# Four graph-attention layers on one core: reordering the opening, PE transposes for entry 1, and new due times

## The chip, the cores and the metric

The kernel runs on one core of one Trainium2 chip. The metric is the device time of one launch in microseconds. The profile that is quoted is one execution of the program, taken by the hardware profiler. PE is the matmul engine, PEld its weight load, DVE the vector engine, ACT the scalar engine, POOL the GpSimd engine, SP the engine whose queue issues most DMAs.

## What is computed

The input `x` has 16 entries of 1024 nodes with 256 features; `adj` is one 1024 x 1024 adjacency matrix for all of them. Four layers follow one another, each of this form:

```
h = relu(layernorm(x))
x = x + activation(softmax(mask(scores(h))) @ (h @ W))
```

Layers 0 and 3 have four heads of 64 features, and their scores are `leaky_relu(s_src + s_dst)` with two numbers per node and head. Layer 1 is the same with one head of 256. Layer 2 has full products `(h W1)(h W2)^T` as scores. Layers 0, 1 and 3 end with elu, layer 2 with relu.

## The kernel before

Everything is fp32. The weight of a pair of nodes is factored, so that the exponential of a leaky relu becomes a maximum of a row value and a column value: one DVE instruction (L1117 for layers 0 and 3, L1208 for layer 1) makes one *p tile*, 128 keys x 512 queries, masked by the transposed adjacency (`mask`, four quarters). PE multiplies it with the values: for a head of layers 0 and 3 into `acc` (eight key tiles, 16 narrow matmuls of 65 columns in the trace for each tile), for layers 1 and 2 into `accb` (257 columns). Layer 2's tiles come from a PE product (`qT`, `hT`, 512 columns), two exponentials on ACT (L1235, L1236) and two DVE instructions (L1240, L1241). One entry has 128 tiles of p for layers 0 and 3 together, 16 for layer 1 and 16 for layer 2.

Before each layer stands a prologue: statistics on DVE (L822, L823), the reciprocal root as a POOL power (L858), `nshift` on DVE (L861), normalised tiles `h` on ACT (L891), their transposes, the projection with the layer's weight on PE, and its eviction on ACT (L972, L975, L977 or L983 on DVE). The transposes go one of two ways. In the usual way ACT splits `h` into 16-bit planes (L914), a DMA turns them (L918), and ACT puts them together (L932). In the *direct* way PE turns `h` as fp32 tiles (L906) and ACT copies them (L929); there, too, the rows of row values come by PE from one column each (L1025) and an ACT copy (L1029), not through DRAM (L1051, L1064). Before, entry 0's layer 0 and the last entry's layer 3 go the direct way.

No engine's order is written by hand. Each step is given to a `Plan` with an engine, a cost, a due time, the steps it follows and the buffers it takes; the plan simulates the engines and, for each of them, picks the step with the earliest due time among those that are ready. What comes out is the order in which instructions are issued; at run time, engines wait on one another's semaphores, not on the plan. Due times are in periods of 190 us: `START` for a layer's tiles, `LEAD` for how long ahead its prologue is due, `STEP` between its pairs of tiles, `WHEN` for layers 1 and 2, and `LATER` and `AHEAD` for single entries near both ends. Buffers matter too: 8 of p, 18 of p1 (layers 1 and 2), 5 of x (the four adjacency quarters take four of them at the start), 2 each of `acc` and `accb`, 1 of `o`.

The program opens with the loads of entry 0's x in three parts (L636, on SP), the four adjacency quarters of 1 MB (L729, on SP), and w0 with its a vectors on ACT's queue (L654, L664). w0 gets extra columns (DVE, L674, L684, L697) for the scores, and the adjacency becomes the mask: compare (L737, DVE), transpose (PE, L595), copy (L750).

Of the kernel before, what the change touches and what calls it, by code (L numbers as in the profile page):

```python
# [44 lines left out]

PERIOD, EARLY = 190.0, 0.7407
START = {0: 0.0, 1: 1.0372, 2: 2.297, 3: 3.5524}  # L50
LEAD = {0: 0.7046, 1: 0.4612, 2: 0.2956, 3: 1.6786}
STEP = {0: 0.01, 1: 0.0686, 2: 0.0892, 3: 0.0445}
WHEN = {
    (1, "weights"): ((-0.5242, 0.0026), (-0.1464, 0.0419)),
    (1, "attended"): ((0.7567, 0.0147), (0.2574, 0.106)),
    (2, "weights"): ((-0.0331, 0.0103), (0.3531, 0.0135)),
    (2, "attended"): ((0.642, 0.0926), (0.4636, 0.0079)),
}

LATER = {  # L60
    (1, 0): 0.596, (1, 1): 0.958, (13, 2): 0.03, (13, 3): 0.392, (14, 3): -0.089, (0, 2): -0.137, (12, 2): 0.2,
    (13, 1): -0.61, (13, 0): 0.042, (0, 1): 0.165, (14, 2): 0.012, (12, 3): 0.381, (15, 2): 0.061,
    (14, 1): 0.153, (0, 3): -0.204, (0, 0): 0.005, (15, 1): 0.169, (3, 0): -0.106, (3, 2): -0.226,
    (3, 1): -0.037, (3, 3): 0.253, (14, 0): -0.403, (15, 3): 0.422, (12, 0): 0.216, (2, 2): -0.002,
    (2, 3): -0.052, (12, 1): -0.053, (1, 3): 0.022,
}
AHEAD = {
    (1, 0): 0.818, (15, 3): 0.338, (12, 1): 1.914, (15, 1): 0.404, (1, 3): -1.162, (0, 3): 0.168,
    (14, 2): 0.163, (14, 1): -0.3, (1, 1): -0.058, (0, 2): 0.142, (13, 1): 0.271, (3, 1): 0.197, (14, 3): 0.426,
    (3, 3): -0.404, (2, 2): 1.115, (15, 0): -0.042, (12, 0): 0.12, (1, 2): 0.321, (2, 3): -0.168,  # L70
    (3, 2): -0.354, (2, 1): -0.221, (13, 3): -0.364, (0, 1): 0.057, (12, 3): 0.014, (0, 0): -0.016,
    (13, 2): -0.254,
}
# [466 lines left out]
def fast(  # L540
# [16 lines left out]
    nc = tc.nc  # L557
    B, N, F = x.shape
    NT = N // P
# [85 lines left out]
    def weight(w, name, due, a=None, heads=0, own=1):  # L645


        t = const.tile([P, KC, F + 2 * heads], F32, name=name)

        first = name == "w0"  # L650
        queue, engine = (nc.scalar, ACT) if first else (nc.sync, SP)

        def load():
            queue.dma_start(out=t[:, :, :F], in_=w.rearrange("(c p) f -> p c f", p=P))  # L654

        s = landed(plan.add(engine, 0.5, due, load), due, 256)
        if a is None:
            return t, s
        d = F // heads
        tiles = {}  # L660

        def load_a():
            tiles["a"] = buf("p1", [P, own, 2, d], name="a_bc")
            queue.dma_start(  # L664
                out=tiles["a"].rearrange("p h s d -> p (h s d)"),
                in_=bass.AP(tensor=a.tensor, offset=a.offset, ap=[[0, P], [1, own * 2 * d]]),
            )

        s2 = landed(plan.add(engine, 0.5, due, load_a, take=("p1",)), due, own * d)

        def sign():
            for side, by in enumerate((1.0 - SLOPE, SLOPE - 1.0)):
                of = tiles["a"][:, :, side, :]
                nc.vector.tensor_scalar(of, of, by, None, op0=OP.mult)  # L674

        s2 = plan.add(DVE, 0.4, due + 0.5, sign, (s2,))
        done = []
        for c in range(KC):

            def columns(c=c):  # L680
                wa = tiles["wa", c] = buf("u", [P, heads, 2, d], name="wa")
                for side in range(2):
                    of = tiles["a"][:, :, side, :]
                    (nc.vector if first else nc.gpsimd).tensor_mul(  # L684
                        wa[:, :, side, :],
                        t[:, c, :F].rearrange("p (h d) -> p h d", h=heads),
                        of if own == heads else of.to_broadcast([P, heads, d]),
                    )

            m = plan.add(*((DVE, 0.7) if first else (POOL, 2.0)), due + 0.5, columns, (s, s2, *done), take=("u",))  # L690
            done = []
            for hd in range(1 if first else heads):

                def add_up(c=c, hd=hd):
                    wa, to = tiles["wa", c], t[:, c, F:].rearrange("p (s h) -> p h s", s=2)
                    if first:
                        nc.vector.tensor_reduce(to, wa, AX.X, OP.add)  # L697
                        return
                    for side in range(2):
                        junk = small.tile([P, F], BF16, name="junk_a", bufs=1)[:, :d]  # L700
                        nc.scalar.activation(
                            junk, wa[:, hd, side, :], AF.Identity, accum_out=to[:, hd, side : side + 1]
                        )

                give = () if not first and hd < heads - 1 else ("u", "p1") if c == KC - 1 else ("u",)
                done.append(
                    plan.add(*((DVE, 0.6) if first else (ACT, 1.1)), due + 0.5, add_up, (m, *done[-1:]), give=give)
                )
        return t, done[-1]

    first_x = load_x(0, SOON)

# [3 lines left out]

    w0, w0_ready = weight(w_l0, "w0", SOON, a_l0, 4, 4)
    plan.add(ACT, 1.6, SOON, warm)
    plan.add(DVE, 0.2, SOON, lambda: nc.vector.tensor_copy(ident_b, ident))

    def mask_steps():
        done = {}
        for n, (half, jh) in enumerate(((0, 0), (0, 1), (1, 0), (1, 1))):
            due, quarter = 15.0 + n if half else SOON + n, {}

# [4 lines left out]

            loaded = landed(plan.add(SP, 0.9, due, load, take=("x",)), due, 1024)
            for t in range(HT):
# [5 lines left out]

                s = plan.add(DVE, 0.45, due, positive, (loaded,), take=("h",), give=("x",) if t == HT - 1 else ())

# [10 lines left out]

                s = plan.add(*((ACT, 0.6) if half else (DVE, 0.45)), due, keep, (s,), give=("pp",))
                done.setdefault((half, jh), []).append(s)
# [11 lines left out]
    def w12_steps(due):  # L765
        tiles, last = {}, []
        for k, w in enumerate((w1_l2, w2_l2)):
# [4 lines left out]

            loaded = landed(plan.add(SP, 0.5, due, load, take=("p1",)), due, 256)
            for cc in range(KC):
# [53 lines left out]
    class Layer:  # L828
# [7 lines left out]
        def prologue(self, due, step, stats, direct=False):  # L836
# [12 lines left out]
            for n, its in enumerate(slice(*part) for part in parts):  # L849
# [28 lines left out]

                at = due - (len(parts) - n - 1)
                s = plan.add(DVE, 0.2, at, norm, (*stats[its], ready[-1] if n else None))  # L880
                s = plan.add(POOL, 2.0, at, norm2, (s,))
                take = () if n else (tag,) if self.gat else (tag, "hq")
                ready += [plan.add(DVE, 0.2, at, norm3, (s,), take=take)] * (its.stop - its.start)
            copies, evicted = [], []
            for n, t0 in enumerate(range(0, NT, 2)):
# [37 lines left out]
                def kept(t0=t0):  # L923
                    if self.gat:
                        T["hT", t0] = buf("hTp", [P, KC, 2 * P])
                    else:
                        T["hT", t0] = self.hT[:, :, t0 * P : (t0 + 2) * P]
                    if direct:
                        nc.scalar.copy(T["hT", t0], T["tp", t0])  # L929
                        return  # L930
# [3 lines left out]
                take = ("hTp",) if self.gat else ()  # L934
                if direct:
                    s = plan.add(PE, 0.47, at, turned, (s,), take=("pp",), give=("h", "h"), wide=True)
# [8 lines left out]
                for k in range(2):  # L945
# [40 lines left out]
                    cost = 0.32 if many or not self.gat else 0.65 if heads == 1 else 1.05  # L986
                    s2 = plan.add(ACT, cost, at, evict, (s2,), give=() if many else ("pp",))
                    if many:
                        s2 = plan.add(DVE, 0.43, at, scaled, (s2,), give=("pp",))
# [27 lines left out]
            if direct:  # L1017
                for half in range(2):
                    for hd in range(heads):
# [7 lines left out]
                        def keep(half=half, hd=hd):  # L1027
# [3 lines left out]
                        s = plan.add(  # L1031
                            PE, 0.44, at + (half * heads + hd) * 0.01, spread, tuple(evicted[half * HT : (half + 1) * HT]),
                            take=("pp", f"row{heads}"), wide=True,
                        )
                        self.row_ready[half, hd] = plan.add(ACT, 0.6, at, keep, (s,), give=("pp",))
                return
# [16 lines left out]

            s = plan.add(PE, 0.14, at, factors, tuple(evicted), take=("pp",))
            s = plan.add(ACT, 0.35, at, keep, (s,), give=("pp",))
# [336 lines left out]
    for start, b, layer in sorted(order):  # L1392
# [5 lines left out]
        elif b:  # L1398
            loads[b] = load_x(b, due - 0.45 * PERIOD, tuple(lays[b - 1, 0].ready))
            stats = [statistics(b, t, due, (loads[b][t],)) for t in range(NT)]  # L1400
        else:
            due, step = SOON, 0.1
            stats = [statistics(b, t, due - 2.5 + t // 2 * 0.9, (loads[b][t],)) for t in range(NT)]
        lay.prologue(due, step, stats, direct=(b, layer) in ((0, 0), (B - 1, 3)))
# [70 lines left out]
```

## Time and profile before

| | |
|---|---|
| median of 3 runs | 2980.43 us (2977.99 to 2980.48) |
| span of the profiled run | 2977.1 us |
| mean clock granted to PE | 0.993 |
| PE busy | 2911.8 us, 98% |
| DVE busy | 2645.6 us, 89% |
| ACT busy | 1922.3 us, 65% |
| p tiles of layers 0 and 3 (L1117) | 2048, 768 ns each |
| 65-column matmuls on them | 32768 |

A busy share is a mean over stages with different limits. What a change at the opening is worth has to be read from the opening, from which engine waits there and for what. Times in the timeline count from the start of the span.

### The profile page before, as it was taken

Reading aid. Unit: us, or ns where it says so; the run is one execution under the profiler, and the core shown is the slowest. Engines: PE = TensorE matmul, PEld = TensorE weight load, DVE = VectorE, ACT = ScalarE, POOL = GpSimd, SP = SyncE. Lnnn points to the kernel's source line nnn. Section 1 sums busy time; section 2 is a strip of 40 time slices with the busy share of each in tenths; the row PEclk is TensorE's granted clock in tenths of the full one; section 3 lists DMA queues with packets and bytes.
Section 4 is the critical chain, followed back from the end, with each engine's and each line's share of the span. In section 5 each row is a group of like instructions: output and inputs, shape, how many; then the busy total and the mean of one; then the engine's idle time right before and its main releaser. Section 6 shows DMA issues by size and latency. Waiting matters only on the chain.

```text
span 2977.1 us, 108647 instructions
## 1 busy us (share of the span) xinstructions
PE 2911.8 (98%) x47954; PEld 2321.2 (78%) x47954; DVE 2645.6 (89%) x5286; ACT 1922.3 (65%) x4776; POOL 234.5 (8%) x151
## 2 busy tenths in 40 slices
PE   7899999999999999999999999999999999999997
PEld 5776868779697887878779787786877869796876
DVE  8989988899898899989899898988999999797698
ACT  6767776785655767566775656766656684656543
POOL 2111100000000000000000100000000010000001
PEclk9899999999999999999999999999999999999999
DMA  4422223333232333313233232331413332121210
GB/s 130 94 55 59 66 48 97 69 63 74 47 71 58 69 73 59 80 40 84 48 66 77 48 78 44 74 71 38 92 40 70 76 63 57 41 57 35 52 36 25
DMA packets 344048, 188.06 MB, mean 63 GB/s; under 512 B 268880, under 2 KB 304400, under 8 KB 343568
## 3 DMA queue, kind: packets, MB, share of 16 engines
q1 hardware_dynamic: 343152, 180.51, 27.1%
q8 instruction: 378, 6.19, 0.9%
q14 instruction: 102, 0.84, 0.1%
q10 hardware_dynamic: 416, 0.52, 0.1%
HBM read 98.63 MB, written 17.33 MB: 39 GB/s over the span
## 4 chain that ended last, share of the span: by engine, by line
PE 84%; DVE 12%; ACT 1%; issue 1%; DMA 0%; POOL 0%; SPq 0%; DVEq 0%; POOLq 0%
PE pp L582 31%; PE accb L582 27%; PE acc L582 26%; DVE p L1117 8%; DVE o L1088 1%; DVE bn L822 1%; DVE xt L1090 0%; DVE p L1241 0%; DVE mv L823 0%; DVE p L1240 0%; DMA xt<-in_x_dram 0%; ACT hTp L932 0%; POOL xt L1097 0%; DMA turned<-planes 0%; DVE rden L1150 0%
## 5 line engine op out<-in xcount | busy, mean ns | idle before, releaser
L1117 DVE SCALAR_TENSOR_TENSOR p<-row,ke,mask 128x512 f32<-128x512 f32 x2048 | 1460.3, 768 | 34.2 <-PE acc L582 32.6
L582 PEld LDWEIGHTS acc<-val,p 128*64 128x64 f32 x32768 | 1072.4, 139 | 121.6 <-issue 47.3
L582 PE MATMUL acc<-val,p 128*64 128x65 f32 x32768 | 1074.5, 223 | 38.9 <-DVE p L1117 33.8
L582 PE MATMUL accb<-val,p 128*64 128x257 f32 x8192 | 928.0, 380 | 0.0
L582 PEld LDWEIGHTS accb<-val,p 128*64 128x64 f32 x8192 | 734.4, 136 | 131.6 <-issue 4.1
L582 PE MATMUL pp<-qT,hT 128*64 128x512 f32 x2048 | 461.4, 592 | 0.0
L582 PE MATMUL pp<-w,hTp 128*64 128x264 f32 (+1 forms) x3072 | 380.8, 386 | 3.3 <-ACT hTp L932 2.1
L582 PEld LDWEIGHTS pp<-qT,hT 128*64 128x64 f32 x2048 | 171.1, 137 | 211.9 <-issue 209.2
L582 PEld LDWEIGHTS pp<-w,hTp 128*64 128x64 f32 x3072 | 242.5, 137 | 85.2 <-issue 12.0
L891 ACT ACTIVATE h<-xt,nshift,rstd 128x256 f32<-128x256 f32 x512 | 275.5, 596 | 38.2 <-DVE nshift L861 38.2
L1240 DVE SCALAR_TENSOR_TENSOR p<-u,p 128x512 f32<-128x512 f32 x256 | 175.7, 686 | 127.5 <-ACT p L1236 127.1
L1275 ACT ACTIVATE o<-accb,rdens 128x256 f32<-128x256 f32 x128 | 60.5, 473 | 346.9 <-DVE rdens L1267 340.5
L914 ACT COPY planes<-h 128x512 uint16<-128x512 uint16 x496 | 281.8, 621 | 0.0
L932 ACT COPY hTp<-turned 128x1024 uint16<-128x1024 uint16 x184 | 214.2, 1168 | 30.0 <-DMA turned<-planes 29.9
L822 DVE BATCH_NORM_STATS2 bn<-xt 128x6 f32<-128x256 f32 x512 | 211.8, 414 | 13.3 <-DMA xt<-in_x_dram 5.4
L1235 ACT ACTIVATE u<-pp 128x512 f32<-128x512 f32 x256 | 152.9, 597 | 104.7 <-PE pp L582 79.3
L1164 ACT ACTIVATE o<-acc,rden 128x64 f32<-128x64 f32 x572 | 132.2, 316 | 113.4 <-DVE rden L1150 99.9
L858 POOL TENSOR_TENSOR rstd<-rstd,neg_half 128x8 f32<-128x8 f32 (+2 forms) x67 | 124.5, 1858 | 976.0 <-DVE rstd L855 643.2
L1241 DVE TENSOR_TENSOR p<-p,mask 128x512 f32<-128x512 f32 x256 | 179.2, 700 | 8.8
L1097 POOL TENSOR_TENSOR xt<-xt,o 128x1024 f32<-128x1024 f32 x35 | 97.5, 2785 | 1131.7 <-DVE o L1088 1009.6
L1208 DVE SCALAR_TENSOR_TENSOR p<-row,ke,mask 128x512 f32<-128x512 f32 x256 | 180.2, 738 | 0.6 <-DMA row<-er_d 0.5
L977 ACT ACTIVATE val<-pp,val 128x64 f32<-128x64 f32 (+1 forms) x640 | 179.4, 347 | 0.0
(87 smaller groups left out, 1911.7 us busy)
## 6 DMA issues: line engine op xcount, KB each, us to landing
row<-er_d SPq DMA_DIRECT2D x272, 256.0 KB, 3.6
xt<-in_x_dram SPq DMA_DIRECT2D x31, 512.0 KB, 4.8
out_dram<-xt SPq DMA_DIRECT2D x31, 512.0 KB, 3.4
raw<-in_adj_dram SPq DMA_DIRECT2D x4, 1024.0 KB, 15.6
raw<-in_adj_dram SPq DMA_DIRECT2D x16, 256.0 KB, 3.4
turned<-planes SPq DMA_TRANSPOSE x248, 3.2
xt<-in_x_dram SPq DMA_DIRECT2D x2, 256.0 KB
w<-in_L_gnn_W_dram SPq DMA_DIRECT2D x2, 256.0 KB
```

Source lines behind the costliest of these rows:

```text
L582: nc.tensor.matmul(to[c : c + COLS], stationary[:, c : c + COLS], moving, start=start, stop=stop, skip_group_check=True,)
L822: nc.vector.bn_stats(st, x_tiles[b][:, t, :])
L891: nc.scalar.activation(h, x_tiles[b][:, t, :], AF.Relu, bias=T["shift"][:, t : t + 1], scale=T["rstd"][:, t : t + 1],)
L914: nc.scalar.copy(to[:, :, :, k, :], of)
L932: nc.scalar.copy(bits, T["tp", t0].rearrange("p s c q -> p c q s"))
L977: nc.scalar.mul(to[:, hd, :], of[:, hd, :], a[:, hd, :])
L1117: nc.vector.scalar_tensor_tensor(p, lay.rows[half, hd], lay.ke[:, lay.heads + hd, jt : jt + 1], mask_of(half, jt), op0=OP.max, op1=OP.mult)
L1164: nc.scalar.mul(to[:, t, :], acc[:, t, :d], rden[:, t, :])
L1208: nc.vector.scalar_tensor_tensor(p, lay.rows[half, 0], lay.ke[:, 1, jt : jt + 1], mask_of(half, jt), op0=OP.max, op1=OP.mult)
L1235: nc.scalar.activation(u, e, AF.Exp, scale=1.0 - SLOPE)
L1240: nc.vector.scalar_tensor_tensor(p, u, 1.0, p, op0=OP.max, op1=OP.mult)
L1241: nc.vector.tensor_mul(p, p, mask_of(half, jt))
```

## The change

It has five parts.

1. The opening is ordered anew: x is due ahead of all else, the function table of ACT is loaded before w0, the adjacency and the later weights come after x in the plan, and entry 0's norms are due earlier. The costs given for POOL's power, the mask's steps and two others are set anew.
2. The second half of w0's score columns is multiplied on POOL, not on DVE.
3. Entry 1's layer 0 is turned on PE as fp32 tiles, as entry 0's is (its rows still go through DRAM, its values are still scaled on ACT).
4. Rows and row factors depend, in the plan, on the step that makes the factors, and no longer on the scaling of the values after it; in the direct way the first half's rows are due earlier.
5. With these, all due times are searched anew.

The aim is an opening in which PE gets work sooner, and a schedule that fits it. The diff, cut to its core:

```diff
+TURNED_ON_PE = ((0, 0), (1, 0), (15, 3))
-PERIOD, EARLY = 190.0, 0.7407
-START = {0: 0.0, 1: 1.0372, 2: 2.297, 3: 3.5524}
-LEAD = {0: 0.7046, 1: 0.4612, 2: 0.2956, 3: 1.6786}
-STEP = {0: 0.01, 1: 0.0686, 2: 0.0892, 3: 0.0445}
+PERIOD, EARLY = 190.0, 0.8675
+START = {0: 0.0, 1: 0.9913, 2: 2.3055, 3: 3.7048}
+LEAD = {0: 0.5044, 1: 0.6878, 2: 0.5749, 3: 1.5128}
+STEP = {0: 0.0066, 1: 0.0345, 2: 0.1367, 3: 0.0242}
...
-        s = landed(plan.add(engine, 0.5, due, load), due, 256)
+        begin = () if first else tuple(mask_ready[0, 0])
+        s = landed(plan.add(engine, 0.5, due, load, begin), due, 256)
...
-            def columns(c=c):
+            def columns(c=c, at_once=first and c == 0):
...
-                    (nc.vector if first else nc.gpsimd).tensor_mul(
+                    (nc.vector if at_once else nc.gpsimd).tensor_mul(
...
-    first_x = load_x(0, SOON)
+    first_x = load_x(0, SOON - 10.0)
...
-    w0, w0_ready = weight(w_l0, "w0", SOON, a_l0, 4, 4)
-    plan.add(ACT, 1.6, SOON, warm)
+    plan.add(ACT, 1.6, SOON - 9.0, warm)
+    w0, w0_ready = weight(w_l0, "w0", SOON - 6.0, a_l0, 4, 4)
...
-            due, quarter = 15.0 + n if half else SOON + n, {}
+            due, quarter = 15.0 + n if half else -1.5 if jh else SOON - 5.2, {}
...
-            loaded = landed(plan.add(SP, 0.9, due, load, take=("x",)), due, 1024)
+            loaded = landed(plan.add(SP, 0.9, due, load, (first_x[2 if n == 0 else -1],), take=("x",)), due, 1024)
...
-                at = due - (len(parts) - n - 1)
+                at = due - 5.0 * (len(parts) > 1)
                 s = plan.add(DVE, 0.2, at, norm, (*stats[its], ready[-1] if n else None))
-                s = plan.add(POOL, 2.0, at, norm2, (s,))
+                s = plan.add(POOL, 0.6 + 0.17 * (its.stop - its.start), at, norm2, (s,))
...
+            on_pe = (b, layer) in TURNED_ON_PE
...
-                if direct:
+                if on_pe:
                     s = plan.add(PE, 0.47, at, turned, (s,), take=("pp",), give=("h", "h"), wide=True)
                     s = plan.add(ACT, 0.6, at, kept, (s,), take=take, give=("pp",))
...
-            s = plan.add(PE, 0.14, at, factors, tuple(evicted), take=("pp",))
+            s = plan.add(PE, 0.14, at, factors, tuple(factored), take=("pp",))
...
-            due, step = SOON, 0.1
-            stats = [statistics(b, t, due - 2.5 + t // 2 * 0.9, (loads[b][t],)) for t in range(NT)]
+            due, step = SOON - 5.0, 0.1
+            stats = [statistics(b, t, due - 2.5 + t // 2 * 0.5, (loads[b][t],)) for t in range(NT)]
```

`WHEN`, `LATER` and `AHEAD` get new numbers throughout as well.

## The prediction

> **What bounds the kernel now.** First the page's busy shares and its 40 slices:
> ```profile
> PE 2911.8 (98%) x47954; PEld 2321.2 (78%) x47954; DVE 2645.6 (89%) x5286; ACT 1922.3 (65%) x4776; POOL 234.5 (8%) x151
> ...
> PE   7899999999999999999999999999999999999997
> ...
> DVE  8989988899898899989899898988999999797698
> ```
> The reader is to see that PE is full in every slice but the first two and the last (74 us each). So I cut the span by stage; columns are length, busy time of PE, PE's weight load, DVE, ACT and POOL, the granted clock, DMA share, GB/s:
> ```profile
> 0.00:20.00 20.00, 5.97 (x52) 3.69 (x54) 12.55 (x41) 5.98 (x11) 3.47 (x12) 1.00 0.92 317
> 20.00:60.00 40.00, 37.05 (x694) 29.18 (x692) 38.02 (x82) 28.27 (x90) 6.38 (x6) 1.00 0.32 75
> 60.00:100.00 40.00, 27.37 (x656) 24.01 (x654) 37.75 (x69) 25.04 (x98) 11.75 (x7) 0.87 0.19 55
> 100.00:140.00 40.00, 36.34 (x854) 32.74 (x850) 37.72 (x67) 35.88 (x99) 5.10 (x3) 0.92 0.47 85
> ...
> 180.00:220.00 40.00, 35.55 (x583) 24.74 (x581) 28.88 (x55) 34.03 (x71) 6.59 (x5) 0.87 0.43 75
> ...
> 300.00:1300.00 1000.00, 996.60 (x16122) 802.80 (x16119) 894.57 (x1836) 679.53 (x1673) 73.64 (x46) 1.00 0.30 67
> ...
> 2904.00:2977.00 73.00, 56.74 (x1339) 50.24 (x1338) 62.31 (x110) 24.68 (x71) 11.78 (x3) 0.91 0.08 25
> ```
> Three stages: an opening to about 200 us in which DVE is 94-95% busy and PE waits for its p tiles; a middle, 99.7% PE; an end where DVE leads again. PE's waits over the whole span say the same:
> ```profile
> PE acc L582 <- DVE p L1117: 33.8, 34, 8.3
> PE pp L906 <- ACT h L891: 11.9, 1, 11.9
> PE acc L582 <- ACT o L1164: 3.9, 1, 3.9
> ```
> 22.0 of the 33.8 us fall before 300 us, 5.5 after 2850, about 6.4 between. The 11.9 us is the wait for the first normalised tile. Two moments in the timeline matter, the first p tile and the last layer's start:
> ```profile
> 25.78 3.42 DVE L1117 SCALAR_TENSOR_TENSOR p<-row,ke,mask 128x512 f32<-128x512 f32 x3
> ...
> 32.76 4.73 DVE L1117 SCALAR_TENSOR_TENSOR p<-row,ke,mask 128x512 f32<-128x512 f32 x7
> ```
> ```profile
> 2904.05 0.17 DVE L1267 RECIPROCAL rdens<-accb 128x1 f32<-128x1 f32 x1 [2.40 <-PE accb L582]
> ...
> 2911.80 2.74 DVE L1117 SCALAR_TENSOR_TENSOR p<-row,ke,mask 128x512 f32<-128x512 f32 x4
> ...
> 2922.82 7.49 POOL L1097 TENSOR_TENSOR xt<-xt,o 128x1024 f32<-128x1024 f32 x1 [15.17 <-DVE o L1088]
> ...
> 2931.32 5.70 PE L582 MATMUL acc<-val,p 128*64 128x65 f32 x112 [3.93 <-ACT o L1164]
> ```
> Wait brackets name the engine waited for.
>
> **What the Trainium skill says.** "SBUF — State Buffer", "SBUF: two separate sides": VectorE and GpSimd hold a shared port pair in turn for a whole instruction. The trace agrees: four p tiles took 5.71 us from 69.30, while the POOL add of 68.71 ran, and 2.73 us elsewhere. "TensorE: Matmul & The Clock Gate", "What's actually happening": an idle array falls to half clock. The trace agrees in direction: 0.87 after the 8.3 us wait before 97 us. "DMA: Bandwidth & Descriptors", "Queues, rings and completion order": DMA engines take turns between queue rows, so w0 on ACT's queue shares bandwidth with x on SP's. That fits x's second part, first used at 7.96 us, 3.55 us after the first.
>
> **The change, part by part.**
> *Opening loads.* ACT loads its function table (1.28 us) before it issues w0 and the a vectors, so these start near 3.3 us instead of 0.74; 0.5 MB less competes with x. At the 317 GB/s of the first row that is 1.6 us for x's later parts. SP issues x and the four adjacency quarters in the same order as before; their new dependencies live in the planner only. I take x complete by 8.5 us instead of 9.5.
> *w0's second product* goes from DVE (2 x 0.415 = 0.8 us) to POOL (2 x 1.144 = 2.3 us). POOL starts it after its last norm, at about 12.7, and ends at 15.0; DVE's reduce then ends at 16.3. Beside it run the four mask comparisons.
> *First p tile.* In the new order PE does six projections (0.9 us each) and three row spreads before it, against four and two. 16.3 + 5.5 + 0.6 (spread) + 0.6 (ACT's row copy) gives 23.2 us against 25.78; from both sides 21.7 (adjacency early) and 24.5 (w0 late). But DVE has then done 3.0 us less work: new order 14.9 us, old 17.9 us by the same rows. The opening is mostly reordered.
> *To the peak.* I count DVE work in program order with back-to-back spacings read from the timeline (p tile 0.70, bn_stats 0.41, aggregate 0.12, o 1.19). Entry 0's layer 2 is what lets PE catch up. Up to its first projections DVE does 144 layer-0 tiles and 16 of layer 1 before, 141 and 16 after; 56 statistics each in both. The sums are 176.5 and 173.7 us. From the tile that starts at 32.76 (sum 23.8) 152.7 us remain; in the new order its counterpart (sum 21.8) starts by my chain at 30.6 and 151.9 us remain. The waits and port delays that DVE adds in between (from 32.76 + 152.7 = 185.5 to the real 191.8) I keep: 6.3 us. So this point moves from 191.8 to 188.8: **-3.0 us**.
> *Entry 1 by PE transposes.* Eight DMA-transposed ACT splits (0.62 each) go; four ACT copies shrink from 1.17 to 0.59; PE gains 16 transposes, 4 x 0.6 = 2.4 us. These lie in the opening, where PE waits for DVE: nothing on the path, and no transpose wait saved, since DVE has entry 0's tiles to do meanwhile.
> *Middle.* Matmuls are the same in number and PE is full: nothing to gain but the 6.4 us of p waits. From the peak to the last accb product PE has 2688.7 us of work in the new order, 2688.8 in the old. Against PE work, with eight p buffers, DVE's work in the new order runs behind in three short stretches, by 0.8, 2.4 and 0.5 us; in the old by 0.3. I charge a third of the difference: **+1.0**.
> *End.* In the new order the last entry's first four tiles are projected after the last accb product, and six leftover tiles of entry 14 hold p buffers. Working the chain from that product: first p tile at 8.6 us (before 7.75), first head's eighth at 17.0 (before 15.5), the POOL add from 21 (before 18.8). If POOL's add takes 2.8 us (its mean) rather than 7.49, the 3.93 us wait does not come: 72.2 us to the end against 73.0; if it takes 7.49, 75.3. I take **+0.8**.
> Sum: -3.0 + 1.0 + 0.8 = -1.2; 2980.4 - 1.2 = 2979.2, said as 2979.0.
>
> **Rivals.** *Faster.* The first p tile comes at 21.7 (-1.5), DVE's own waits between 26 and 196 us (rden on PE 2.9, ex on ACT 1.3, buffers 1.0: 5.2 us) vanish, the end gains 0.8, the middle loses nothing: -3.0 - 1.5 - 5.2 - 0.8 = -10.5, 2970. For it: fresh due times may close those waits. Against it: DVE's count hardly falls.
> *Slower.* A new order brings p waits in the middle: the 3.7 us above, and its many stretches with under 1 us to spare each losing a little, 4 more; the end costs 2.3; the opening gains nothing because PE, with three more projections and 16 transposes early, comes within 2 us of being late itself. 2980.4 + 10 = 2990. For it: from 2130 to 2400 us the new order leaves DVE no spare time.
> *A hidden opening.* x lands earlier but adjacency bounds DVE: first p at 24.5, so -1.7, and 2980.5; this falls in the same band as my forecast.
>
> **How the numbers follow.** The forecast has 0.27, the hidden opening 0.12, together 0.39 within 0.2% (6 us); the faster rival 0.36, the slower 0.25. Each rival can go about 6 us beyond its figure (the POOL hold, another round of waits), hence 2964 to 2992, to leave out no more than 2 in 10.
>
> **What would show it.** Right: the first p tile near 23 us, the wait of PE for p before 300 us at 18-21 us, the middle at 99.5% or more, last accb product to end 72-75 us. Wrong: a first p tile under 21 or over 25; p waits in the middle over 12 us; DVE waits near zero up to 190 us; or a middle in which ACT or transposes end PE's waits.

## The result, and the profile after

The changed kernel takes 2991.98 us (median of 4 runs, 2990.72 to 2993.87), the kernel before 2979.21 us beside it (4 runs, 2977.50 to 2980.48). The ratio is 1.0044, 95% interval 1.0026 to 1.0061: slower by about 0.4%. The profiled spans are 2988.9 and 2977.1 us, with the same mean clock, 0.993.

The page of the changed kernel, busy time and two rows of its slices:

```profile
PE 2926.7 (98%) x47970; PEld 2294.2 (77%) x47970; DVE 2650.8 (89%) x5284; ACT 1914.7 (64%) x4768; POOL 229.6 (8%) x153
...
PE   7799999999999999999999999999999999999997
...
DVE  8978897979999889999899898999989999974888
```

PE stays full from the third slice on, and nothing on this page tells where 12 us went. The windows by stage, columns as before:

```profile
0.00:20.00 20.00, 7.87 (x68) 5.30 (x70) 12.94 (x41) 7.62 (x17) 4.62 (x14) 1.00 0.91 318
20.00:60.00 40.00, 37.04 (x680) 30.06 (x676) 36.59 (x78) 23.04 (x80) 3.68 (x3) 0.96 0.25 81
60.00:100.00 40.00, 28.16 (x646) 24.36 (x648) 37.12 (x69) 22.72 (x94) 12.55 (x9) 0.91 0.08 23
100.00:140.00 40.00, 36.35 (x860) 31.22 (x857) 38.23 (x67) 33.95 (x94) 5.95 (x4) 0.97 0.46 87
...
300.00:1300.00 1000.00, 995.16 (x16175) 784.45 (x16173) 896.57 (x1815) 675.96 (x1665) 72.18 (x45) 1.00 0.30 67
```

PE's waits over the whole span, and the moments of the timeline that answer to those of before (first p tile, first projection of entry 0's layer 2, the end of the last `accb`, the first p tile after it, the POOL add). The projection's line of the kernel before stands ahead of those of the changed kernel:

```profile
PE acc L585 <- DVE p L1127: 39.6, 35, 5.7
PE pp L915 <- ACT h L900: 11.7, 2, 10.5
```

```profile
195.59 5.15 PE L582 MATMUL pp<-w2v,hT 128*64 128x256 f32 x32
```

```profile
24.19 2.08 DVE L1127 SCALAR_TENSOR_TENSOR p<-row,ke,mask 128x512 f32<-128x512 f32 x3 [0.48 <-ACT row L1039]
...
198.53 5.20 PE L585 MATMUL pp<-w2v,hT 128*64 128x256 f32 x32
...
2916.44 0.17 DVE L1277 RECIPROCAL rdens<-accb 128x1 f32<-128x1 f32 x1 [1.61 <-PE accb L585]
...
2924.62 2.08 DVE L1127 SCALAR_TENSOR_TENSOR p<-row,ke,mask 128x512 f32<-128x512 f32 x3 [1.22 <-ACT row L1039]
...
2937.07 2.86 POOL L1107 TENSOR_TENSOR xt<-xt,o 128x1024 f32<-128x1024 f32 x1 [17.47 <-DVE o L1098]
```

The first p tile comes 1.6 us sooner, yet layer 2 of entry 0 begins 2.9 us later. The tail is 72.5 us from the last `rdens` (73.0 before).

The wait view doesn't account for the loss: between 400 and 2850 us it lists 4.3 us of waits for p, against 6.4 before. So I count what PE has done. *Lost time* at a moment is the time elapsed less that of the matmuls begun by then, each at its back-to-back spacing in an undisturbed run of its kind: 29.1 ns for 65 columns, 108.75 for 257, 112.0 for 264, 109.5 for 258, 108.5 for 256, 214.8 for 512; the fp32 transposes of `h` count nothing, so that both kernels are measured by the same useful work. The small products of other kinds (of the mask and of the rows) are counted too; they make 22 us by the end, alike in all columns. The record holds every matmul (32768 of 65 columns, 8192 of 257 in both). The other columns belong to experiments below (e14, e1; e10, e15, e6).

```
lost by (us)  before  after | opening  code,   | add on DVE:
                            | alone    old due |  before  opening  after
  100          41.5    42.1 |  43.0    41.9    |   41.1    42.5    41.5
  300          62.2    66.9 |  63.3    65.2    |   56.7    56.7    60.9
  400          63.0    72.1 |  67.0    68.9    |   56.7    58.8    65.1
  700          64.2    72.5 |  72.8    74.5    |   56.8    63.2    64.8
 1000          66.0    77.0 |  72.9    74.5    |   56.7    63.8    67.1
 2000          70.8    87.7 |  77.8    78.6    |   57.4    64.7    68.9
 2850          77.0    90.6 |  83.8    83.8    |   59.1    66.8    69.2
  end         107.7   119.5 | 114.3   115.5    |   84.6    91.9    94.0
```

The 11.8 us between the spans are: 4.7 by 300 us, 4.4 from 300 to 400, 4.5 from there to 2850, and 1.8 won back at the end. The middle's 4.5 is a balance: between 1000 and 2000 us the changed kernel loses 10.7 us, the one before 4.8; from 2000 to 2400 it is 0.9 against 6.1.

The largest single stall, in the timeline of the changed kernel (DVE, POOL and PE):

```profile
369.53 5.50 DVE L1127 SCALAR_TENSOR_TENSOR p<-row,ke,mask 128x512 f32<-128x512 f32 x5
369.61 2.88 POOL L1107 TENSOR_TENSOR xt<-xt,o 128x1024 f32<-128x1024 f32 x1 [14.47 <-DVE o L1098]
...
373.09 2.77 PE L585 MATMUL acc<-val,p 128*64 128x65 f32 x64 [0.55 <-DVE p L1127]
374.95 0.41 DVE L830 BATCH_NORM_STATS2 bn<-xt 128x6 f32<-128x256 f32 x1
...
377.14 5.36 DVE L1127 SCALAR_TENSOR_TENSOR p<-row,ke,mask 128x512 f32<-128x512 f32 x8
377.92 0.69 PE L585 MATMUL acc<-val,p 128*64 128x65 f32 x16 [1.99 <-DVE p L1127]
378.44 2.88 PE L585 MATMUL pp<-w2v,hT 128*64 128x256 f32 x16
```

Five p tiles beside the add take 5.50 us (3.37 elsewhere), four statistics follow at once, PE has no tile left and waits 0.55 and 1.99 us. Then it pays again: 16 projections take 2.88 us, against 1.90 at 385.07. The granted clock, third figure from the end of a window's line, is 0.92 and then 0.74:

```profile
375.00:380.00 5.00, 2.94 (x50) 2.15 (x48) 4.86 (x15) 3.62 (x11) 0.00 (x0) 0.92 0.82 109
380.00:385.00 5.00, 5.00 (x118) 4.45 (x116) 4.01 (x8) 4.51 (x9) 0.00 (x0) 0.74 0.44 106
```

### The profile page after: what moved, and what is told of

It reads as the page before. It is cut to its first block, busy times and chain, and to the rows that moved or that the text cites. A ratio compares the mean times of both kernels' runs of the same rounds, so it can differ in the third digit from the quotient of the medians.

```text
span 2988.9 us, 108737 instructions
## 1 busy us (share of the span) xinstructions
PE 2926.7 (98%) x47970; PEld 2294.2 (77%) x47970; DVE 2650.8 (89%) x5284; ACT 1914.7 (64%) x4768; POOL 229.6 (8%) x153
## 4 chain that ended last, share of the span: by engine, by line
PE 86%; DVE 11%; issue 1%; ACT 1%; DMA 1%; SPq 0%; DVEq 0%; ACTq 0%
PE pp L585 30%; PE accb L585 29%; PE acc L585 27%; DVE p L1127 7%; DVE bn L830 1%; DVE p L1250 1%; DVE p L1251 1%; DVE o L1098 1%; DVE mv L831 0%; DMA turned<-planes 0%; DMA xt<-in_x_dram 0%; DVE rden L1160 0%; PE pp L915 0%; ACT h L900 0%; PE pp L1035 0%
## 5 line engine op out<-in xcount | busy, mean ns | idle before, releaser
L585 PE MATMUL acc<-val,p 128*64 128x65 f32 x32768 | 1094.6, 224 | 40.7 <-DVE p L1127 39.6
L585 PEld LDWEIGHTS accb<-val,p 128*64 128x64 f32 x8192 | 712.5, 137 | 158.5 <-issue 7.1
L585 PE MATMUL pp<-qT,hT 128*64 128x512 f32 x2048 | 471.2, 593 | 0.0
L585 PEld LDWEIGHTS pp<-qT,hT 128*64 128x64 f32 x2048 | 159.4, 137 | 187.3 <-issue 179.8
L1098 DVE SCALAR_TENSOR_TENSOR o<-ex,o 128x256 f32<-128x256 f32 (+1 forms) x195 | 131.6, 676 | 53.8 <-ACT ex L1094 53.4
```

The source lines that it names most:

```text
L585: nc.tensor.matmul(to[c : c + COLS], stationary[:, c : c + COLS], moving, start=start, stop=stop, skip_group_check=True,)
L1098: nc.vector.scalar_tensor_tensor(o, ex, -1.0, o, op0=OP.mult, op1=OP.max)
```

## The experiments

All are compared with the kernel before on the same chip; the ratio is to it. Where the table above has a column, its numbers are used.

**1. Due times or code?** The tables of due times were exchanged, whole or in halves.

```diff
# e1: the changed code            e2: the code before
-PERIOD ... AHEAD of the change   -PERIOD ... AHEAD of before
+PERIOD ... AHEAD of before       +PERIOD ... AHEAD of the change
# e3: only PERIOD/EARLY, START, LEAD, STEP, WHEN of before in the changed kernel
# e4: only LATER, AHEAD of before in the changed kernel
```

> The changed code (opening, entry 1 turned by PE) with every due time of the kernel before. Theory T1, the due times lose the time: 2976 to 2981 us, PE's stretch 300-2850 us as full as before, the first p tile still near 24 us. Rival T2, the new opening and the PE transposes lose it: 2989 to 2993 us. A third way, that code and times fit only each other: above 2993 us here and in the run with the old code.

> The code before with every due time of the changed kernel. T1: 2988 to 2994 us, with the stall near 375 us and small waits for p all through the middle. T2: 2977 to 2982 us.

> The changed kernel with START, LEAD, STEP, WHEN and EARLY of before, its own LATER and AHEAD. If the loss lies in the steady period (about 1.2 us for each of the entries in the middle by PE's records): 2980 to 2985 us. If it lies in the stall near 375 us and in the opening, which LATER and AHEAD of the first entries set: 2988 to 2994 us. T2: 2989 to 2993.

> The changed kernel with LATER and AHEAD of before and its own START, LEAD, STEP, WHEN and EARLY: the other half. If LATER and AHEAD lose the time (stall near 375 us 5 us, opening 4): 2981 to 2986 us. If the steady period does: 2987 to 2993 us, and the stretch 700-2000 us no fuller than in the changed kernel. T2: 2989 to 2993.

Measured: e1 2986.73 us (1.0026, 1.0016 to 1.0037), e2 2997.47 (1.0064, 1.0050 to 1.0078), e3 3035.14 (1.0191, 1.0177 to 1.0205), e4 2991.51 (1.0039, 1.0026 to 1.0053). No theory holds in its pure form: the code alone costs 7.8 us against 2978.93 us before, the new due times alone, on the old code, 18.5, and both together 12.8 (against 2979.21). The halves don't go with one another: e3 loses 17 us between 700 and 1000 and 26 between 2000 and 2850 us, where one table hands over to the other. But one thing is clean. Between 1000 and 2000 us every kernel with the old steady tables loses 4 to 5 us (before 4.8, e1 4.1, e3 4.7), every one with the new tables 8 to 11 (after 10.7, e2 10.4, e4 8.5).

**2. The residual add on POOL.** The stall above suggested it.

```diff
# e6, at its planned place in the order; the planner still counts it as POOL 2.7 us
-lambda: nc.gpsimd.tensor_add(xs(), xs(), T["o", key])
+lambda: nc.vector.tensor_add(xs(), xs(), T["o", key])
# e13, the planner told of it
-s = plan.add(POOL, 2.7, due, lambda: nc.gpsimd.tensor_add(...), (s,), give=gives)
+s = plan.add(DVE, 1.2, due, lambda: nc.vector.tensor_add(...), (s,), give=gives)
# e12 (entries 0 and 1 only), e17 (entries 2 to 13 only)
+lambda: (nc.vector if self.b < 2 else nc.gpsimd).tensor_add(...)
+lambda: (nc.vector if 2 <= self.b < 14 else nc.gpsimd).tensor_add(...)
# e9, less work for DVE instead
-nc.vector.bn_stats(st, x_tiles[b][:, t, :])
+nc.vector.bn_stats(st, x_tiles[b][:, t, : F // 2])
```

> The changed kernel, in which the residual add of layers 0 and 3 (128x1024, 35 times) is issued on DVE instead of POOL, at the same place of the order. Theory P, the add on POOL stretches p tiles through the shared port (five took 5.50 us at 133.66 and at 369.53, against 3.37 elsewhere) and so causes the stalls near 140 and 375 us: both stalls shrink, 2981 to 2986 us. Rival D, DVE simply has too much to do there: 35 adds of about 1.2 us more, stalls as large or larger, 2990 to 2998 us.

> The changed kernel with statistics taken over 128 of the 256 columns (the norm is then another one): about 0.13 us less DVE work in each of 512 statistics, the order of all engines unchanged. Theory S, PE's small losses in the middle are waits for p tiles, that is for DVE: the time that PE loses against its matmul work between 1000 and 2000 us falls from 10.7 us to under 7, and the total to 2976 to 2985 us. Rival, PE's new order costs it by itself (more changes between kinds of matmul): 2987 to 2992 us, 10 us lost as before.

e6: 2964.38 us (0.9950, 0.9933 to 0.9966), better than either theory had it, and faster than both kernels. DVE does 35 instructions more and is busy *less*: 2621.5 us against 2650.8. The timeline of e6 near its 132 us:

```profile
131.32 0.72 DVE L1127 SCALAR_TENSOR_TENSOR p<-row,ke,mask 128x512 f32<-128x512 f32 x1
131.96 1.22 DVE L1107 TENSOR_TENSOR xt<-xt,o 128x1024 f32<-128x1024 f32 x1
133.10 2.74 DVE L1127 SCALAR_TENSOR_TENSOR p<-row,ke,mask 128x512 f32<-128x512 f32 x4
```

An add costs DVE 1.22 us here (1.14 to the next instruction). On POOL its *hold*, the time by which it lengthens the DVE instruction beside it, is 2.1 us. Over all 35 adds of the changed kernel the holds sum to 69 us, the adds on DVE to 40; the difference is the 29 us that DVE is less busy. The stall near 140 us shrinks (lost by 160 us: 54.7 to 51.0, 50.9 before); the one near 370 us does not go (4.3 us of 5.4 stay), so there theory P failed: without a hold, four statistics in a row ahead of the p tiles are still followed by a wait of 1.99 us, and by slow projections:

```profile
370.96 0.97 PE L585 MATMUL acc<-val,p 128*64 128x65 f32 x16 [1.99 <-DVE p L1127]
...
371.72 3.33 PE L585 MATMUL pp<-w2v,hT 128*64 128x256 f32 x16
```

Between 1000 and 2000 us e6 loses 1.8 us in place of 10.7.

e9: 2976.98 us (0.9995, 0.9986 to 1.0004); 5.3 us lost between 1000 and 2000 us. Its statistics take 281 ns each in place of 414, in the groups view. PE's order is the changed kernel's in both, so PE's small losses are waits for DVE, too short for the wait view; the rival (PE's order as such) falls. One thing e6 does not separate: the add on DVE also gives back `o`, which has one buffer, sooner. On ACT the changed kernel lists 10.5 us of waits for the POOL add, but on PE none for `o`, so I take its share to be small; e9, which leaves the adds on POOL, gains 15 us.

> The changed kernel with the add on DVE in entries 0 and 1 alone. If the hold near 133 and 369 us makes those two stalls and the middle's loss comes from the later adds: the time lost by 400 us falls from 72 to about 65 us, the loss of 10 us between 1000 and 2000 us stays, 2981 to 2986 us in all. If the middle's loss is a consequence of the late start: it vanishes too, under 2976 us.

> The changed kernel with the residual add on DVE in entries 2 to 13 only; the first two and last two entries keep it on POOL, so the late start (67 us lost by 300 us, 72 by 400) stays. Theory H, in the new order both adds of an entry hold a p tile (4.1 us a period, against about 2.1 before, where one of them fell beside statistics), and that alone makes the middle's loss: the loss between 1000 and 2000 us falls from 10.7 us to under 2.5, 2971 to 2977 us in all. Rival, the middle's loss needs the late start too, or comes from the new order itself: over 5 us lost there, 2980 us or more.

> As the changed kernel with the add on DVE, but with the planner told of it (DVE 1.2 us), so that all orders are drawn up anew. If only the hold counts: 2960 to 2968 us. If the new order brings waits of its own: 2970 to 2985 us.

e12: 2987.92 us (1.0029, 1.0018 to 1.0040), just above its forecast: 66.4 us lost by 400 us in place of 72.1, but still 10.5 between 1000 and 2000. e17: 2974.95 (0.9986, 0.9978 to 0.9993): 70.7 by 400 us, and only 1.8 between 1000 and 2000. So the loss between 1000 and 2000 us belongs to the middle's adds, with or without a late start. e13: 2986.60 (1.0023, 1.0013 to 1.0033), just above its slower forecast: the same work, but an order drawn up anew, and it is 22 us behind e6; it loses 11 us between 1800 and 2000 and again between 2400 and 2600. The due times fit one order, and telling the planner the truth unfits them.

Why does the same add cost more after than before? The timelines show what stands beside it. Before, in the middle of the run:

```profile
1450.12 2.37 POOL L1097 TENSOR_TENSOR xt<-xt,o 128x1024 f32<-128x1024 f32 x1 [26.56 <-DVE o L1088]
1450.63 0.42 DVE L822 BATCH_NORM_STATS2 bn<-xt 128x6 f32<-128x256 f32 x1
1451.08 0.18 DVE L823 BATCH_NORM_AGGREGATE mv<-bn 128x2 f32<-128x6 f32 x1
1451.18 0.40 DVE L822 BATCH_NORM_STATS2 bn<-xt 128x6 f32<-128x256 f32 x1
```

and the changed kernel, in the same place of the period:

```profile
1467.86 2.38 POOL L1107 TENSOR_TENSOR xt<-xt,o 128x1024 f32<-128x1024 f32 x1 [31.24 <-DVE o L1098]
1468.36 2.43 DVE L1127 SCALAR_TENSOR_TENSOR p<-row,ke,mask 128x512 f32<-128x512 f32 x1
```

Statistics run beside the add at their usual 0.40 us; a p tile is held, 2.43 us here, up to 2.87. Each entry has two such adds. Between 900 and 1710 us, in the old order one of the two in a period (919, 1105, 1271, 1450, 1629 us) fell beside statistics and held DVE by 0 to 0.7 us; in the new order all ten held it, by 1.7 to 2.1 us. The sum over the adds between 1000 and 2000 us, each DVE instruction beside one less the median of its kind, is 24.5 us after (12 adds) and 15.3 before (11).

**3. Entry 1 turned by PE.**

```diff
# e7: the changed kernel                        # e8: the kernel before
-TURNED_ON_PE = ((0, 0), (1, 0), (15, 3))       -if direct:
+TURNED_ON_PE = ((0, 0), (15, 3))               +if direct or (b, layer) == (1, 0):
```

> The changed kernel with entry 1's layer 0 turned by DMA again (splits on ACT). If the PE transposes of entry 1 are hidden in the opening, as the prediction said: 2988 to 2994 us. If they or the order they bring cost the 3 us by 160 us: 2984 to 2987 us.

> The kernel before with only entry 1's layer 0 turned on PE, its due times kept. If hidden: 2977 to 2982 us. If the transposes cost time by themselves: 2983 to 2988 us, with the loss ahead of 200 us.

e7: 2992.62 us (1.0047, 1.0030 to 1.0063), no different from the changed kernel's 1.0044. e8: 2981.39 (1.0009, 1.0002 to 1.0015), a cost of 3 us in the old order, between 0.6 and 4.5 by its interval. In the changed kernel the transposes are hidden; there this part is neither gain nor cause.

**4. Both orders without the hold.** The edit of e6, in the kernel before (e10) and in e1 (e11).

> The kernel before with the residual add of layers 0 and 3 issued on DVE, at the same place of the order. Theory P, the POOL adds make the difference between the two sets of due times (29 p tiles over 1.5 us in the changed kernel, 24 in the one before): the kernel before gains clearly less than the 27.6 us of the changed one, 2963 to 2970 us, so that the two come out within 4 us of one another. Rival, the new due times lose time of themselves: 2950 to 2956 us, the two still 10 us apart.

> The changed code with every due time of before and the add on DVE. P: 2962 to 2971 us, near the changed kernel with the add on DVE (2964.4). Rival, the old due times are better with or without the hold: 2955 to 2960 us.

e10: 2957.19 us (0.9924, 0.9911 to 0.9938), the fastest of all: 23 us faster than the kernel before, 35 faster than the changed one. e11: 2963.74 (0.9949, 0.9935 to 0.9962). The old order gains 23.2 us from the edit, the new 27.6, so the result lies between the theories: of the 12.8 us, 7 to 9 stay without any hold. The lost time says where these lie (e6 less e10): 4.2 us by 300 us and 6.2 from there to 1000; after it e6 wins 1.0 us back. On the new code the due times now hardly differ (2963.74 with the old, 2964.38 with the new; 5.3 us apart with the hold). The middle of e10 is all but free of loss: 56.7 us lost by 1000, 59.1 by 2850.

**5. The opening alone.** The changed code with the old due times, entry 1 by DMA and the rows after `evicted` as before (e14); e15 adds the edit of e6. e16 is e6 with LATER and AHEAD of before for entries 0 to 3.

```diff
-TURNED_ON_PE = ((0, 0), (1, 0), (15, 3))
+TURNED_ON_PE = ((0, 0), (15, 3))
-at - 2.5 * step * (1 - half) + ..., spread, tuple(factored[...])
+at + ..., spread, tuple(evicted[...])
-plan.add(PE, 0.14, at, factors, tuple(factored), take=("pp",))
+plan.add(PE, 0.14, at, factors, tuple(evicted), take=("pp",))
```

> The kernel before with the new opening alone (x, warm-up, w0 and masks in the new order, second product on POOL, statistics and norms first); entry 1 by DMA, rows after the scaled value, all due times of before. The prediction gave the opening 3 us: 2976 to 2978 us. If the opening only reorders DVE's work and the rest follows: 2979 to 2983 us. If it upsets what the due times of before were made for: 2984 to 2988 us.

> The same with the add of layers 0 and 3 on DVE. The kernel before with that add takes 2957.2, the changed code with old due times 2963.7. If the opening carries what the structure loses: 2962 to 2966 us. If it is the other edits (entry 1 on PE, rows from the first factor): 2955 to 2959 us.

> The changed kernel with the add on DVE and LATER and AHEAD of the entries 0 to 3 from before. If the stall near 370 us, which stays without any POOL add (4.3 us between 350 and 400), belongs to these due times: that stretch loses under 1.5 us and the total is 2956 to 2962 us, unless the mixed due times bring another stall. If it belongs to the steady due times or the code: it stays, 2962 to 2968 us.

e14: 2983.53 us (1.0018, 1.0011 to 1.0025), at the edge between its second and third forecast; e15: 2963.81 (0.9954, 0.9940 to 0.9967), the same as e11. By 300 us the opening has won nothing: 56.7 us lost in e15 and in e10. What it costs comes later, 6.5 us between 300 and 700, in places like this one of e15's timeline:

```profile
520.57 0.69 DVE L1251 TENSOR_TENSOR p<-p,mask 128x512 f32<-128x512 f32 x1
521.18 1.41 DVE L1218 SCALAR_TENSOR_TENSOR p<-row,ke,mask 128x512 f32<-128x512 f32 x2
521.32 4.13 PE L585 MATMUL accb<-val,p 128*64 128x257 f32 x36 [2.15 <-DVE p L1251]
```

PE waits 2.15 us for layer 2's last masked tile, which stands behind six other p tiles, a residual add and a statistic in DVE's order; e10 lists no wait at all between 400 and 1000 us. e16: 2969.36 us (0.9967, 0.9955 to 0.9979); the stall between 350 and 400 us is gone (0.4 us lost there, 4.3 in e6), so it belongs to these due times (e4, with LATER and AHEAD of before throughout, loses 1.2 us there, e2, with the new ones on the old code, 5.0). But the mixed tables lose 5.6 us by 140 us more and 7.4 between 500 and 700.

## Why the prediction was wrong

The forecast was 2979 us; its slower rival, 2990, is near what came, and two of its reasons hold: p waits with a little lost in many places, and an opening that gains nothing. That its sum fits is in part luck. It gave the middle 7.7 us (8.9 came) and the opening none (4.7 were lost by 300 us), and it counted 2.3 us for a longer end, which did not come. The place that it named, 2130 to 2400 us, is not where the loss lies (0.9 us from 2000 to 2400), and the transposes that it blamed in the opening are hidden (e7). Most signs that the prediction named could not tell it from a right one: the first p tile, the end, and a middle at 99.5% (995.16 of 1000 us) came as for a right forecast. Only the p waits before 300 us, 25.0 us in place of 18 to 21, spoke against it. Step by step:

*Opening loads.* The premise was wrong, the result nearly right. ACT issued w0's load at 1.47 us, inside its table load (0.74 to 2.02), not at 3.3:

```profile
0.74 1.28 ACT L722 ACT_TABLE_LOAD   x1 [0.74 <-PEq L1466]
...
1.47 0.44 ACTq L657 DMA_DIRECT2D w<-in_L_gnn_W_dram  x1
```

x's last part was first used at 9.12 us (9.48 before, 8.5 forecast), the first p tile came at 24.19 (23.2 forecast, though the terms written there add to 23.0; within the bounds).

*To the peak, -3.0 us.* This step failed: the point moved by +2.9 (layer 2's first projection, 195.59 to 198.53 us). Up to the tile that answers to that of 32.76 us it was right: forecast for 30.6, this tile began at 30.69.

```profile
30.69 4.06 DVE L1127 SCALAR_TENSOR_TENSOR p<-row,ke,mask 128x512 f32<-128x512 f32 x6
```

The count of tiles was right too (three fewer than before). What failed is "the waits and port delays that DVE adds in between I keep: 6.3 us". DVE's waits from 24 to 196 us, before and then after:

```profile
DVE rden L1150 <- PE acc L582: 2.9, 3, 1.1
DVE o L1088 <- ACT ex L1084: 1.3, 1, 1.3
DVE p L1117 <- PE acc L582: 1.0, 2, 0.6
```

```profile
DVE o L1098 <- ACT ex L1094: 2.9, 2, 1.4
DVE p L1127 <- PE acc L585: 2.3, 5, 0.6
DVE p L1127 <- ACT val L981: 1.3, 1, 1.3
DVE rden L1160 <- PE acc L585: 1.2, 3, 0.5
DVE rden L1277 <- PE accb L585: 0.9, 3, 0.3
DVE p L1127 <- ACT row L1039: 0.5, 1, 0.5
```

5.2 us became 9.1: DVE, given its tiles sooner, stood waiting for PE and ACT. The 6.3 us had also been read too small, because a tile was priced at 0.70 us; the seven of 32.76 us begin 0.66 us apart (4.73 us less one tile's 0.74, over six). Counted with such spacings, from that tile to the end of the last p tile ahead of the projection, DVE's back-to-back work is 144.3 us of 159.0 before and 143.4 of 163.8 after. So it adds 14.7 us before and 20.4 after. Of the 5.7 us more, 3.6 are waits, 1.0 is time of instructions held beside a POOL instruction, and 1.1 is in smaller gaps. They turn a gain of 3.0 us into a loss of 2.7, counted on DVE. Free of the hold, and with old due times, the opening brought that projection forward by 1.2 us (191.34 in e10, 190.14 in e15), and by 300 us by nothing.

*Entry 1 by PE transposes*, nothing: right for the changed kernel (e7); alone in the old order it costs about 3 us (e8).

*Middle, +1.0 us.* The largest error: from 300 to 2850 us the changed kernel loses 23.7 us, the one before 14.8, +8.9. The step compared DVE's work with PE's at back-to-back times of 0.70 us a tile, found stretches in which DVE runs behind, and charged a third of them. Two things failed.

From 300 to 1000 us the changed kernel loses 10.1 us and the one before 3.8; without the hold (e6 and e10) it is 6.2 and nothing. So these 6 us are the new order itself, and 4.3 of them are the stall near 370 us, four statistics in a row ahead of the p tiles. If that stall is one of the step's stretches, which the record does not show, a third was too small a charge: PE waited 2.5 us there, and the slower clock added about 1 us to it.

From 1000 to 2000 us the changed kernel loses 5.9 us more than the one before, and without the hold 1.1. Here the step left out the 2.1 us by which each POOL add holds a p tile, though the prediction itself had read that hold in the opening and at the end. (Of its 5.71 us for four tiles, only the first tile, 2.77 us, was held by that add; two more took 1.22 us each beside another POOL product, at 71.47.) "SBUF — State Buffer", section "SBUF: two separate sides", of the Trainium skill says which DVE work is held: an instruction with two inputs in SBUF, against a GpSimd instruction that reads SBUF, or one in a two-port mode. The traces agree on the first: p tiles (row and mask) are held, statistics (one input) are not. One `rstd` step with a single input, at 94.63 us before, took 1.86 us in place of 0.17 beside an add, which fits the second. With that read before, the question for the new order would have been what stands beside each add.

After 2000 us the balance turns: to 2850 the kernel before loses 3.3 us more than the changed one.

*End, +0.8 us.* It came out at -0.5 (72.5 against 73.0). The first p tile came 8.2 us after the last `rdens` (8.6 forecast), and the POOL add took 2.86 us: the branch worked out as 72.2 is the one that happened.

Two things stay open. I have not shown why an opening that is the same by 300 us leads the planner to another order at 520 us; only that it does (e15). And the loss by 300 us without a hold is split only in the large: 56.7 us before (e10) and with the new opening (e15), 57.9 with all of the new code (e11), 60.9 with the new due times as well (e6). Which table of due times costs these 3.0 us is not shown, since half tables bring stalls of their own (e3, e4, e16), and the new due times on the old code were not run without the hold.

## What to carry to other kernels

When two engines share a port, look at which instruction of the other engine runs beside each long one: the same 35 adds cost 23 us in one order and 28 in the other, and moving them to the engine they held was worth more than either set of due times. Judge a full engine by the work it has done by a moment, not by its busy share or its listed waits. A schedule searched for one order of work is worth little for another: a small edit at the start, a table exchanged by half, or a corrected cost each brought new stalls hundreds of microseconds later.

## What the runs showed of the hardware that was not expected

PE's busy time can rise while its work falls. The window from 1000 to 2000 us, before, after and in e6:

```profile
1000.00:2000.00 1000.00, 996.84 (x16733) 813.07 (x16730) 915.64 (x1831) 654.27 (x1599) 74.53 (x44) 1.00 0.30 66
```

```profile
1000.00:2000.00 1000.00, 997.96 (x16692) 788.42 (x16690) 911.84 (x1813) 659.07 (x1642) 73.99 (x45) 1.00 0.29 64
```

```profile
1000.00:2000.00 1000.00, 999.95 (x16822) 801.53 (x16820) 909.99 (x1838) 660.17 (x1636) 43.48 (x33) 1.00 0.29 64
```

The changed kernel is busier than the one before, 997.96 against 996.84 us, and lost 5.9 us more in it. Of the 10.7 us that it lost there, only 2.0 show as idle.

The length of a wait alone does not tell whether the clock falls. After waits of 0.55 and 1.99 us near 375 us the granted clock was 0.74 in a 5 us window, and in e6, after 1.99 us alone, 0.66 (370 to 375 us). But the wait of 2.15 us in e15, before 521.32 us, left it at 1.00, and so did one of 2.07 us before 2940.53 us in the changed kernel. What makes the difference is not shown.

And ACT issued its next DMA 0.73 us into a table load of 1.28 us, without waiting for its end.
